# Graph network layer on one core: 72 directly summed columns as three bf16 addends, code copies on POOL, four last groups and a shared last norm

## The chip, the cores and the metric

The kernel runs on one core of a Trainium2 chip. A core has five engines with queues of their own, which run side by side: PE (TensorE, matrix products), DVE (VectorE), ACT (ScalarE), POOL (GpSimd, which also issues the indirect transfers that scatter rows by index) and SP (SyncE, which here issues all other transfers). The metric is the device time of one execution in microseconds, as the median of several runs.

## The reference

206,250 edges carry 128 features each, and 6,250 nodes have 128 features. Every edge's features are added to the node that `src` names; the sums go through three dense layers, and the result plus `x` is normalised over its features. Inputs and output are float32.

```python
edge_aggr = jnp.zeros((n, HIDDEN), dtype=x.dtype).at[row].add(edge_features)
reps = n // global_feat.shape[0]
global_expand = jnp.repeat(global_feat, reps, axis=0)
combined = jnp.concatenate([x, edge_aggr, global_expand], axis=-1) @ W_c + b_c
h = jax.nn.softplus(combined @ W1 + b1)
h = jax.nn.softplus(h @ W2 + b2)
return h @ W3 + b3
...
x = _layernorm(x + _L0_gnn_ref(x, edge_index, edge_attr_128, ...), axis=-1)
```

Negative and out-of-range indices are handled as that scatter-add does it. The edges come in no order that the kernel may rely on.

## The kernel before

**Columns.** The edges are laid over 128 partitions, so that one "column" is 128 edges, one on each; there are 1,612 columns (the last has 42 edges). They are summed in one of two ways.

**Direct columns (48).** `direct_steps` takes them in sets of 12. A set is loaded by one transfer of 768 KB (`load`). For each of 13 windows of 512 nodes (the last has 256) and each pair of columns, ACT makes two 128x512 tables of ones and zeros (`compare`, L577 and L579: is this edge's node this number?), and PE multiplies the rows by them (`add`, L589), in float32, which shows as two records for each product. After the 12 columns of a window DVE adds the result to `sums_t`, the transposed node sums of 128 x 6400 (L593). `compare` runs two steps ahead of `add`; four buffers hold the tables.

**Scattered columns (1,564).** They go through memory in ten groups of `GROUPS`: 40, 120, 200, 240, 240, 240, 212, 140, 88 and 44 columns. The nodes are cut into 25 blocks of 256. For each group:

- `node_codes` (DVE) splits each edge's node into a block and a code inside the block, and `positions` (DVE and PE) counts edges by block and gives every edge a place, so that the edges of one block lie together and each block is padded to a whole number of chunks of `sub` x 128 rows (`sub` is the second number of a group: 1, 2 or 4).
- Pieces of ten columns are loaded by SP (`load_rows`, three pieces ahead, five buffers), ACT copies their ten codes into a 129th value of each row (`code_rows`, L636, issued two pieces ahead), and POOL scatters the rows into a DRAM buffer, one indirect transfer for each column (`scatter_rows`, L644). The DRAM buffer is filled with -1 beforehand (`fill_rows`, on SP), so that padding matches no node.
- `reduce_steps` of the group reads the chunks back, eight chunk columns to a load (SP, L145). DVE compares their codes with 0 to 255 (`match`, L423); PE multiplies the rows by that table (`product`, L437, 256 columns wide, again two records for each); DVE adds each chunk's sum to its block of `sums_t` (L454). In the last two groups (`g > G - 3`) three of every four matches are made by ACT instead (L418 and L420).

**The order of the work.** PE, DVE, ACT and SP have an order written out by hand: while group g is scattered, its loop over pieces deals out, in shares, the preparation of group g+1, the sums of group g-1, the filling for group g+1, the node rows (in groups 3 to 5) and a share of the direct steps (groups 1 to G-4, that is 1 to 6, weighted by `left`). SP's transfers stand in one single order. POOL's queue isn't in that list: the planner places its instructions. The sums of the last group follow after the loop.

**The node layers.** After the last sum, 13 tiles of up to 512 nodes go through the layers. Every few tiles share one `norm`: DVE computes the inverse deviations of all blocks of 128 nodes in a chain of small instructions (L819 to L827), and the blocks are normalised by POOL (L833), in the very last `norm` by DVE. The tiles are parted 4, 3, 3, 2 and 1.

Of the kernel before, what the change touches and what calls it, by code (L numbers as in the profile page):

```python
# [7 lines left out]
F32 = mybir.dt.float32  # L8
# [8 lines left out]
P = 128  # L17
# [4 lines left out]

GROUPS = ((40, 1), (120, 2), (200, 4), (240, 4), (240, 4), (240, 4), (212, 4), (140, 2), (88, 2),
          (44, 1))
CHUNK_ROWS = 1024
PLACES = 3

DIRECT = 48
SET = 12
WIDE = 512  # L30
QUAD = 2
FILL = 4
POS_COLS = 20
# [14 lines left out]
def kernel(  # L48
# [36 lines left out]
    for size, sub in GROUPS:  # L85
        c1 = min(TC, c0 + size)
        if c1 > c0:
# [12 lines left out]

    iota_f = const.tile([P, WIDE], F32, name="iota_f")
    nc.gpsimd.iota(iota_f, pattern=[[1, WIDE]], base=0, channel_multiplier=0,
                   allow_small_or_imprecise_dtypes=True)
# [64 lines left out]
    with ExitStack() as phase:  # L168
# [74 lines left out]
        def positions(g):  # L243
# [5 lines left out]
            in_block, so_far, got = {}, {}, {}  # L249
            pos = per.tile([P, C_MAX], I32, name="pos")  # L250
            pos_of[g] = pos
# [102 lines left out]
            def chunk_map():  # L354

                small = ps.tile([P, 4, P], F32, name="small", bufs=2)
                end_t = per.tile([NB, 1], F32, name="end_t")
                nc.tensor.transpose(small[:NB, 0, :], got["end"], ident)
                nc.vector.tensor_copy(end_t, small[:NB, 0, :1])
                ended = per.tile([NB, NSC_MAX], F32, name="ended")  # L360
                nc.vector.tensor_scalar(ended[:, :nsc], chunk_i[:, :nsc], end_t, None,
                                        op0=ALU.is_ge)
                offs = per.tile([1, NSC_MAX], I32, name="offs", bufs=3)
                offs_of[g] = offs
                flat = ps.tile([P, 4, P], F32, name="small", bufs=2).rearrange("p a b -> p (a b)")
                nc.tensor.matmul(flat[:1, :nsc], ones[:NB, :1], ended[:, :nsc],
                                 start=True, stop=True)
                nc.vector.tensor_scalar(offs[:, :nsc], flat[:1, :nsc], float(NB - 1), float(BL),
                                        op0=ALU.min, op1=ALU.mult)
# [22 lines left out]
        def reduce_steps(g):  # L392
# [16 lines left out]
            def match(i):  # L409
# [3 lines left out]
                hot_of[i] = hot  # L413
                if g > G - 3 and i % 4 != 3:

# [129 lines left out]
        def direct_steps():  # L545


            steps = []
            if not ND:
                return steps  # L550
            NW = -(-NB * BL // WIDE)
            less = keep.tile([P, NW, ND], F32, name="less")
            rows_in, hot_of, sum_of = {}, {}, {}

            def begin():

                first = keep.tile([P, NW], F32, name="first")
                nc.gpsimd.iota(first, pattern=[[WIDE, NW]], base=0, channel_multiplier=0,
                               allow_small_or_imprecise_dtypes=True)
                part, node, _ = whole_nodes(0, ND)  # L560
                nc.vector.tensor_copy(node, part)
                nc.vector.tensor_tensor(
                    less, node.unsqueeze(1).to_broadcast([P, NW, ND]),
                    first.unsqueeze(2).to_broadcast([P, NW, ND]), op=ALU.subtract)

            def load(c):
# [3 lines left out]
                         edge_attr[:P * T, :].rearrange("(p t) d -> p t d", p=P)[:, c:c + n, :])  # L570

            def compare(c, w, q):
                n = min(WIDE, NB * BL - w * WIDE)
                hot = direct_p.tile([P, QUAD, WIDE], F32, name="direct_hot", bufs=4)
                hot_of[c, w, q] = hot
                for j in range(QUAD):
                    nc.scalar.activation(hot[:, j, :n], iota_f[:, :n], AF.Abs,  # L577
                                         bias=less[:, w, c + q + j:c + q + j + 1], scale=-1.0)
                nc.scalar.activation(hot[:, :, :n], hot[:, :, :n], AF.Relu, bias=ones[:, :1],  # L579
                                     scale=-1.0)  # L580

            def add(c, w, q):
# [3 lines left out]
                if q == 0:  # L586
                    sum_of[c, w] = ps.tile([P, WIDE], F32, name="direct_sum", bufs=2)
                for j in range(QUAD):
                    nc.tensor.matmul(sum_of[c, w][:, :n], rows_in[c][:, q + j, :], hot[:, j, :n],  # L589
                                     start=(q + j == 0), stop=(q + j == k - 1))  # L590
                if q + QUAD == k:
# [4 lines left out]
                    for q in range(0, min(SET, ND - c), QUAD)]  # L596
            steps += [begin, lambda: load(0)]
            for i in range(len(jobs) + 2):
                def one(i=i):
                    if i < len(jobs):  # L600
                        c, w, q = jobs[i]
                        if (w, q) == (NW // 2, 0) and c + SET < ND:
                            load(c + SET)
                        compare(*jobs[i])
                    if i > 1:
# [26 lines left out]
        def code_rows(i):  # L632
            if i >= len(pieces):
                return
            g, c, k, r = pieces[i]
            nc.scalar.copy(rows_at[i][:r, :k, D:W], low[:r, c:c + k].unsqueeze(2))  # L636

# [14 lines left out]
        with tc.manual_schedule(engines={ET.PE, ET.DVE, ET.Activation, ET.SP}):  # L652
# [22 lines left out]
            node_codes(ND, c1)  # L675
            for i in range(LEAD - 1):
                code_rows(i)
            for step in positions(0):
# [11 lines left out]
            left = [0.0] * G  # L690
            for g in range(1, G - 3):
                left[g] = max(0.0, groups[g][1] - groups[g][0]
                              - groups[g - 1][3] * groups[g - 1][2] / 3 - (9 if 3 <= g < 6 else 0))
            direct_at = 0.0
            i = 0
            assert G > 6
            nodes = []
            for g in range(G):
                mine = [q for q in range(len(pieces)) if pieces[q][0] == g]
                prep = []  # L700
                if g + 1 < G:
                    prep = [lambda g=g: node_codes(*groups[g + 1][:2])] + positions(g + 1)
                sums = reduce_steps(g - 1) if g else []
# [7 lines left out]
                done = [0, 0, 0, 0]  # L711
                for q in mine:
                    load_rows(i + LEAD)
                    code_rows(i + LEAD - 1)
                    scatter_rows(i)
# [30 lines left out]
    order = tiles[-1:] + tiles[:-1]  # L746
    parts = [order[:4]] + [order[i:i + 3] for i in range(4, len(order) - 3, 3)]
    parts += [order[len(parts) * 3 + 1:-1], order[-1:]]
    h1, h2, sub_z, x_of = {}, {}, {}, {}
# [64 lines left out]
    def norm(now, last):  # L814
# [9 lines left out]
        for _ in range(3):  # L824
            nc.vector.tensor_mul(t, g, g)
            nc.vector.scalar_tensor_tensor(t, t, -0.5, v, op0=ALU.mult, op1=ALU.mult)
            nc.vector.scalar_tensor_tensor(g, t, 1.5, g, op0=ALU.add, op1=ALU.mult)  # L827

        engine = nc.vector if last else nc.gpsimd
        for n0, w, y, at in now["done"]:  # L830
            for lo, hi, r in blocks(w):
                for q in range(lo, hi):
                    engine.tensor_scalar(y[:r, q, :], y[:r, q, :], mv[:r, at + q, 0:1],  # L833
                                         rs[:r, 1, at + q:at + q + 1],
                                         op0=ALU.subtract, op1=ALU.mult)
                m0 = n0 + lo * P
# [60 lines left out]
```

## Time and profile before

| What | Value |
|---|---|
| time, median of 3 runs | 2163.95 us (2160.82 to 2169.29) |
| the profiled execution's own time | 2166.67 us |
| its span | 2164.9 us |
| mean granted PE clock | 0.925 |
| first scatter | 25.57 us |
| PE busy from 1188 to 1296, and from 1296 to 1404 | 98.7 and 92.0 of 108 us |
| POOL busy in the same two | 81.9 and 82.0 of 108 us (86 scatters each) |
| ACT waiting for PE's direct products | 808.1 us in 199 waits |
| SP waiting for PE's chunk products | 885.2 us in 214 waits |
| last matmul of the sums ends / first of the node layers starts | 2084.1 / 2086.1 us |

All lines are of one execution. A busy share is an average over stages with different limits: what decides in a stretch is the engine whose instructions follow each other there without a wait. In a group of instructions, "busy, mean ns of one" comes first and then the idle time of the engine just before them, with what ended it; "issue" is time in which the engine waited for nothing that the profile shows. In a timeline the columns are start, duration, engine, line, operation, output and inputs, count, and in brackets the idle time before with what ended it.

### The profile page before, as it was taken

The page shows a single profiled execution, that of the slowest core. Times are in us where ns is not written, and L with a number is a line of the kernel's source. Part 1 is how long each engine was busy: PE and PEld are TensorE (multiplying, and loading weights), DVE is VectorE, ACT ScalarE, POOL GpSimd, SP SyncE. Part 2 cuts the span into 40 slices and gives each one's busy share as a digit, 9 for nine tenths or more (in the row PEclk, how much of TensorE's full clock was granted, in tenths as well). Part 3 has the DMA queues.
Part 4 walks back from the last instruction along what each step waited for, and adds up shares of the span by engine and source line. Part 5 has one row for each costly group of instructions (what it writes and reads, how often), then busy time and mean ns, then how long its engine had stood idle before and what let it go on. Part 6 is the DMA issues. An engine that isn't in the chain of part 4 may idle for free.

```text
span 2164.9 us, 22230 instructions
## 1 busy us (share of the span) xinstructions
PE 1789.7 (83%) x6415; PEld 1209.0 (56%) x6415; DVE 1328.0 (61%) x1923; ACT 912.7 (42%) x1350; POOL 1560.2 (72%) x1631
## 2 busy tenths in 40 slices
PE   3398788966889878999889998788998899688884
PEld 0144445534555555666556666556666778566752
DVE  7386457524656345675465855355755798796567
ACT  0476665653444335444353443353342000006964
POOL 5777777777777767777777777777777777777226
PEclk8699999987999999999999999999999999899997
DMA  9998788738786665676756666556766687776521
GB/s 299 303 313 270 216 256 251 231 101 262 213 225 189 194 193 148 188 207 188 198 173 180 194 190 175 169 167 189 202 198 170 211 245 227 214 213 199 151 75 60
DMA packets 415376, 435.50 MB, mean 201 GB/s; under 512 B 37743, under 2 KB 305766, under 8 KB 415254
## 3 DMA queue, kind: packets, MB, share of 16 engines
q1 hardware_dynamic: 365062, 330.71, 54.9%
q0 software_dynamic: 50048, 103.35, 14.4%
q8 instruction: 51, 0.84, 0.2%
q14 instruction: 71, 0.58, 0.1%
q10 hardware_dynamic: 144, 0.02, 0.0%
HBM read 260.90 MB, written 173.03 MB: 200 GB/s over the span
## 4 chain that ended last, share of the span: by engine, by line
PE 57%; DVE 15%; POOL 9%; issue 7%; DMA 6%; ACT 4%; DVEq 1%; SPq 0%; POOLq 0%; ACTq 0%
PE part L437 37%; PE direct_sum L589 16%; POOL place L644 8%; DVE hot L423 7%; DMA place<-rows,pos 4%; DVE sums_t L454 2%; ACT hot L418 2%; DVE so_far L316 1%; DVE sums_t L593 1%; DMA rows<-in_edge_attr 1%; DMA chunks<-place 1%; PE small L339 1%; POOL y L833 1%; DVEq L448 1%; DVE pos L350 1%
## 5 line engine op out<-in xcount | busy, mean ns | idle before, releaser
L644 POOL DMA_INDIRECT place<-rows,pos x1564 | 1503.2, 961 | 509.0 <-issue 443.5
L437 PE MATMUL part<-hot,chunks 128*128 128x256 f32 x4472 | 1106.0, 405 | 267.8 <-DVE hot L423 250.9
L437 PEld LDWEIGHTS part<-hot,chunks 128*128 128x128 f32 x4472 | 894.9, 203 | 507.8 <-DVE hot L423 310.5
L577 ACT ACTIVATE direct_hot<-iota_f,less 128x512 f32<-128x512 f32 (+1 forms) x624 | 404.6, 695 | 811.0 <-PE direct_sum L589 808.1
L423 DVE SCALAR_TENSOR_TENSOR hot<-chunks,iota_ps 128x2048 f32<-128x2048 f32 (+1 forms) x261 | 592.2, 2270 | 44.2 <-DMA chunks<-place 44.2
L589 PE MATMUL direct_sum<-direct_hot,direct_rows 128*128 128x512 f32 (+1 forms) x1248 | 559.0, 580 | 29.4 <-DMA direct_rows<-in_edge_attr 25.6
L454 DVE TENSOR_TENSOR sums_t<-sums_t,part 128x256 f32 x781 | 327.1, 419 | 133.3 <-PE part L437 110.8
L589 PEld LDWEIGHTS direct_sum<-direct_hot,direct_rows 128*128 128x128 f32 x1248 | 233.3, 190 | 232.2 <-issue 204.9
L579 ACT ACTIVATE direct_hot<-direct_hot,ones 128x1024 f32<-128x1024 f32 (+1 forms) x312 | 348.0, 1115 | 10.1
L593 DVE TENSOR_TENSOR sums_t<-sums_t,direct_sum 128x512 f32<-128x512 f32 (+1 forms) x52 | 34.7, 667 | 410.5 <-PE direct_sum L589 410.5
L636 ACT COPY rows<-src_i 128x10 f32<-128x10 f32 (+1 forms) x159 | 30.7, 196 | 360.3 <-DMA place<-rows,pos 328.9
L350 DVE TENSOR_REDUCE pos<-at 128x20 int32<-128x500 f32 (+2 forms) x80 | 87.0, 1087 | 2.7
L316 DVE TENSOR_TENSOR_SCAN so_far<-iota_ps,ib 128x1500 bf16<-128x1500 f32 (+5 forms) x29 | 85.7, 2955 | 0.0
L418 ACT ACTIVATE hot<-iota_f,chunks 128x256 f32<-128x256 f32 x156 | 64.2, 493 | 26.7 <-DMA chunks<-place 24.2
L845 POOL TENSOR_TENSOR x_sb<-x_sb,b_all 128x512 f32<-128x512 f32 (+1 forms) x13 | 15.2, 1219 | 67.8 <-DMA x_sb<-in_x 67.8
L348 DVE TENSOR_TENSOR at<-small,ib 128x500 f32<-128x500 f32 (+2 forms) x80 | 52.9, 661 | 4.2 <-PE small L339 3.5
L833 POOL TENSOR_SCALAR y<-y,mv,rs 128x128 f32<-128x128 f32 (+1 forms) x45 | 35.2, 796 | 19.9 <-DVE rs L827 19.0
L262 DVE TENSOR_TENSOR ib<-block,iota_ps 128x1500 bf16<-128x1500 bf16 (+5 forms) x29 | 44.2, 1550 | 0.0
L273 PE MATMUL small<-ib,ones_h 128*128 128x500 bf16 (+2 forms) x80 | 23.8, 406 | 23.9 <-DVE ib L262 23.9
L536 DVE TENSOR_SCALAR z_x<-small,z_bias 128x512 f32<-128x512 f32 (+1 forms) x13 | 9.3, 718 | 51.3 <-PE small L534 51.3
L335 PE MATMUL small<-so_far,ones_h 128*128 128x500 bf16 (+2 forms) x80 | 31.4, 393 | 11.1 <-DVE last L319 11.1
L420 ACT ACTIVATE hot<-hot,ones 128x2048 f32<-128x2048 f32 (+1 forms) x20 | 39.2, 1960 | 0.7
(115 smaller groups left out, 472.7 us busy)
## 6 DMA issues: line engine op xcount, KB each, us to landing
chunks<-place SPq DMA_DIRECT2D x278, 516.0 KB, 4.5
rows<-in_edge_attr SPq DMA_DIRECT2D x155, 640.0 KB, 6.7
place<-fill SPq DMA_DIRECT2D x252, 258.0 KB, 8.3
place<-rows,pos POOLq DMA_INDIRECT x1564, 4.5
x_sb<-in_x SPq DMA_DIRECT2D x24, 256.0 KB, 4.6
direct_rows<-in_edge_attr SPq DMA_DIRECT2D x4, 768.0 KB
out<-y SPq DMA_DIRECT2D x12, 256.0 KB, 2.2
chunks<-place SPq DMA_DIRECT2D x3, 258.0 KB, 3.2
```

The source lines that it names most:

```text
L316: nc.vector.tensor_tensor_scan(t, iota_ps[:, 1:2].to_broadcast([P, NB * n]), in_block[k][0], 0.0, op0=ALU.mult, op1=ALU.add)
L350: nc.vector.tensor_reduce(pos[:, a - c0 + j0:a - c0 + j1], at.rearrange("p b g -> p g b"), axis=mybir.AxisListType.X, op=ALU.add)
L418: nc.scalar.activation(hot[:, j], codes, AF.Abs, bias=chunks[i][:, j, D:W], scale=-1.0)
L423: nc.vector.scalar_tensor_tensor(hot[:, :m], chunks[i][:, :m, D:W].to_broadcast([P, m, BL]), code_of(g), iota_ps.unsqueeze(1).to_broadcast ...
L437: nc.tensor.matmul(part[:, s - q, :], t[:, s * sub + j, :D], hot[:, s * sub + j], start=(j == 0), stop=(j == sub - 1))
L454: nc.vector.tensor_add(here, here, part[:, s - q, :])
L577: nc.scalar.activation(hot[:, j, :n], iota_f[:, :n], AF.Abs, bias=less[:, w, c + q + j:c + q + j + 1], scale=-1.0)
L579: nc.scalar.activation(hot[:, :, :n], hot[:, :, :n], AF.Relu, bias=ones[:, :1], scale=-1.0)
L589: nc.tensor.matmul(sum_of[c, w][:, :n], rows_in[c][:, q + j, :], hot[:, j, :n], start=(q + j == 0), stop=(q + j == k - 1))
L593: nc.vector.tensor_add(here, here, sum_of.pop((c, w))[:, :n])
L644: s = nc.gpsimd.indirect_dma_start(out=dst, out_offset=bass.IndirectOffsetOnAxis(ap=at, axis=0), in_=rows[:r, j, :], in_offset=None)
L833: engine.tensor_scalar(y[:r, q, :], y[:r, q, :], mv[:r, at + q, 0:1], rs[:r, 1, at + q:at + q + 1], op0=ALU.subtract, op1=ALU.mult)
```

## The change

It does five things at once.

1. **72 direct columns instead of 48**, and their products in bf16. A new step `split` (DVE) writes each float32 value as a sum of three bf16 values: its upper 16 bits, the upper 16 bits of what is left, and the rest of that. The first two stand in place in the loaded rows (every second bf16 value of them), the third in a tile of its own. PE multiplies each of the three by the same table, which is now bf16, and adds them in float32 in PSUM. `split` works on two columns at a time, three DVE instructions of 128x256. The difference of node and window start (`less`) is made for a set at a time, and the tables have three buffers after four. The first set's load is issued at the end of group 0, its `begin` and `split` at the start of group 1.
2. **POOL copies the codes** (`code_rows`), called just ahead of the piece's scatters, instead of ACT two pieces ahead.
3. **The last groups** are 202, 130, 72, 38 and 18 columns instead of 212, 140, 88 and 44: eleven groups, 1,540 scattered columns. Direct steps still lie in groups 1 to 6. Matches go to ACT in the last three groups, by `TAIL`: one of two, three of four, three of four.
4. **Positions one group sooner** from group 6 on: group 6 prepares groups 7 and 8, group 7 prepares 9, group 8 prepares 10, with a third `pos` and a fourth `offs` buffer.
5. **The last norm is shared** by the last three tiles (parts of 4, 3, 3 and 3): half of its blocks are normalised by DVE and half by ACT.

```diff
-GROUPS = ((40, 1), (120, 2), (200, 4), (240, 4), (240, 4), (240, 4), (212, 4), (140, 2), (88, 2),
-          (44, 1))
+GROUPS = ((40, 1), (120, 2), (200, 4), (240, 4), (240, 4), (240, 4), (202, 4), (130, 2), (72, 2),
+          (38, 1), (18, 1))
+SOONER = 6
+TAIL = (2, 4, 4)
-DIRECT = 48
+DIRECT = 72
+SPLIT = 2
...
-            pos = per.tile([P, C_MAX], I32, name="pos")
+            pos = per.tile([P, C_MAX], I32, name="pos", bufs=3)
...
-                if g > G - 3 and i % 4 != 3:
+                share = TAIL[g - G] if g >= G - len(TAIL) else 1
+                if i % share != share - 1:
...
+            def halves(t):
+                return [t.bitcast(BF16).rearrange("p c (d h) -> p c d h", h=2)[:, :, :, h]
+                        for h in (0, 1)]
+
+            def split(c):
+                n = min(SET, ND - c)
+                less = less_of[c] = direct_p.tile([P, NW, SET], F32, name="less", bufs=2)
+                nc.vector.tensor_tensor(
+                    less[:, :, :n], node_f[:, c:c + n].unsqueeze(1).to_broadcast([P, NW, n]),
+                    first.unsqueeze(2).to_broadcast([P, NW, n]), op=ALU.subtract)
+                low_in[c] = direct_p.tile([P, SET, D], BF16, name="direct_low", bufs=2)
+                for a in range(0, min(SET, ND - c), SPLIT):
+                    b = min(a + SPLIT, SET, ND - c)
+                    rest = direct_p.tile([P, SPLIT, D], F32, name="direct_rest")[:, :b - a]
+                    x_c = rows_in[c][:, a:b]
+                    nc.vector.tensor_sub(rest, x_c, halves(x_c)[1])
+                    nc.vector.tensor_sub(low_in[c][:, a:b], rest, halves(rest)[1])
+                    nc.vector.tensor_copy(halves(x_c)[0], halves(rest)[1])
...
-                hot = direct_p.tile([P, QUAD, WIDE], F32, name="direct_hot", bufs=4)
+                hot = direct_p.tile([P, QUAD, WIDE], BF16, name="direct_hot", bufs=3)
...
-                for j in range(QUAD):
-                    nc.tensor.matmul(sum_of[c, w][:, :n], rows_in[c][:, q + j, :], hot[:, j, :n],
-                                     start=(q + j == 0), stop=(q + j == k - 1))
+                for j in range(q, q + QUAD):
+                    addends = halves(rows_in[c][:, j:j + 1]) + [low_in[c][:, j:j + 1]]
+                    for i, part in enumerate(addends):
+                        nc.tensor.matmul(sum_of[c, w][:, :n], part[:, 0], hot[:, j - q, :n],
+                                         start=(j == 0 and i == 0), stop=(j == k - 1 and i == 2))
...
+                        if (w, q) == (NW - 2, 0) and c + SET < ND:
+                            split(c + SET)
...
-            nc.scalar.copy(rows_at[i][:r, :k, D:W], low[:r, c:c + k].unsqueeze(2))
+            nc.gpsimd.tensor_copy(rows_at[i][:r, :k, D:W], low[:r, c:c + k].unsqueeze(2))
...
-                if g + 1 < G:
-                    prep = [lambda g=g: node_codes(*groups[g + 1][:2])] + positions(g + 1)
+                for k in range(g + 1 + (g > SOONER), min(G, g + 2 + (g >= SOONER))):
+                    prep += [lambda k=k: node_codes(*groups[k][:2])] + positions(k)
...
+                    if g == 0 and q == mine[-1]:
+                        for step in direct_first:
+                            step()
                     load_rows(i + LEAD)
-                    code_rows(i + LEAD - 1)
+                    code_rows(i)
                     scatter_rows(i)
...
-    parts = [order[:4]] + [order[i:i + 3] for i in range(4, len(order) - 3, 3)]
-    parts += [order[len(parts) * 3 + 1:-1], order[-1:]]
+    parts = [order[:4]] + [order[i:i + 3] for i in range(4, len(order), 3)]
...
+                    if last and q % 2:
+                        nc.scalar.activation(y[:r, q, :], y[:r, q, :], AF.Identity,
+                                             bias=minus[:r, k:k + 1], scale=g[:r, k:k + 1])
+                        continue
```

More of the change, by code (lines that the diff above doesn't have):

```diff
@@ L98 @@
     dram = ctx.enter_context(tc.tile_pool(name="dram", bufs=1, space=bass.MemoryType.DRAM))
-    iota_f = const.tile([P, WIDE], F32, name="iota_f")
-    nc.gpsimd.iota(iota_f, pattern=[[1, WIDE]], base=0, channel_multiplier=0,
+    iota_f = const.tile([P, len(TAIL) * BL], F32, name="iota_f")
+    nc.gpsimd.iota(iota_f, pattern=[[1, len(TAIL) * BL]], base=0, channel_multiplier=0,
                    allow_small_or_imprecise_dtypes=True)
@@ L362, in chunk_map @@
                                         op0=ALU.is_ge)
-                offs = per.tile([1, NSC_MAX], I32, name="offs", bufs=3)
+                offs = per.tile([1, NSC_MAX], I32, name="offs", bufs=4)
                 offs_of[g] = offs
@@ L551, in direct_steps @@
             NW = -(-NB * BL // WIDE)
-            less = keep.tile([P, NW, ND], F32, name="less")
-            rows_in, hot_of, sum_of = {}, {}, {}
+            node_f = keep.tile([P, ND], F32, name="node_f")
+            first = keep.tile([P, NW], F32, name="first")
+            less_of = {}
+            rows_in, low_in, hot_of, sum_of = {}, {}, {}, {}
             def begin():
-                first = keep.tile([P, NW], F32, name="first")
                 nc.gpsimd.iota(first, pattern=[[WIDE, NW]], base=0, channel_multiplier=0,
                                allow_small_or_imprecise_dtypes=True)
[L560 to L564, printed above, removed]
+                part, _, _ = whole_nodes(0, ND)
+                nc.vector.tensor_copy(node_f, part)
             def load(c):
@@ L577, in compare @@
                     nc.scalar.activation(hot[:, j, :n], iota_f[:, :n], AF.Abs,
-                                         bias=less[:, w, c + q + j:c + q + j + 1], scale=-1.0)
+                                         bias=less_of[c][:, w, q + j:q + j + 1], scale=-1.0)
                 nc.scalar.activation(hot[:, :, :n], hot[:, :, :n], AF.Relu, bias=ones[:, :1],
@@ L596, in direct_steps @@
                     for q in range(0, min(SET, ND - c), QUAD)]
-            steps += [begin, lambda: load(0)]
+            steps += [lambda: load(0), begin, lambda: split(0)]
             for i in range(len(jobs) + 2):
@@ L632, in code_rows @@
         def code_rows(i):
-            if i >= len(pieces):
-                return
             g, c, k, r = pieces[i]
-            nc.scalar.copy(rows_at[i][:r, :k, D:W], low[:r, c:c + k].unsqueeze(2))
+            nc.gpsimd.tensor_copy(rows_at[i][:r, :k, D:W], low[:r, c:c + k].unsqueeze(2))
         def scatter_rows(i):
@@ L675 @@
             node_codes(ND, c1)
-            for i in range(LEAD - 1):
-                code_rows(i)
             for step in positions(0):
@@ L690 @@
             left = [0.0] * G
-            for g in range(1, G - 3):
+            for g in range(1, G - 4):
                 left[g] = max(0.0, groups[g][1] - groups[g][0]
                               - groups[g - 1][3] * groups[g - 1][2] / 3 - (9 if 3 <= g < 6 else 0))
+            direct_first = direct[:1]
+            direct = direct[1:]
             direct_at = 0.0
@@ L827, in norm @@
             nc.vector.scalar_tensor_tensor(g, t, 1.5, g, op0=ALU.add, op1=ALU.mult)
-        engine = nc.vector if last else nc.gpsimd
+        if last:
+            minus = work.tile([P, 16], F32, name="minus")[:, :nb]
+            nc.vector.scalar_tensor_tensor(minus, mv[:, :nb, 0], -1.0, g,
+                                           op0=ALU.mult, op1=ALU.mult)
         for n0, w, y, at in now["done"]:
@@ L832, in norm @@
                 for q in range(lo, hi):
-                    engine.tensor_scalar(y[:r, q, :], y[:r, q, :], mv[:r, at + q, 0:1],
-                                         rs[:r, 1, at + q:at + q + 1],
-                                         op0=ALU.subtract, op1=ALU.mult)
+                    k = at + q
+                    if last and q % 2:
+                        nc.scalar.activation(y[:r, q, :], y[:r, q, :], AF.Identity,
+                                             bias=minus[:r, k:k + 1], scale=g[:r, k:k + 1])
+                        continue
+                    (nc.vector if last else nc.gpsimd).tensor_scalar(
+                        y[:r, q, :], y[:r, q, :], mv[:r, k, 0:1], g[:r, k:k + 1],
+                        op0=ALU.subtract, op1=ALU.mult)
                 m0 = n0 + lo * P
```

## The prediction

> **What bounds the kernel now.** I read four views in this order: engine shares, groups of instructions, waits, then POOL's and DVE's timelines at the places that the change touches.
>
> ```profile
> PE 1789.7 (83%) x6415; PEld 1209.0 (56%) x6415; DVE 1328.0 (61%) x1923; ACT 912.7 (42%) x1350; POOL 1560.2 (72%) x1631
> POOL 5777777777777767777777777777777777777226
> L644 POOL DMA_INDIRECT place<-rows,pos x1564 | 1503.2, 961 | 509.0 <-issue 443.5
> L437 PE MATMUL part<-hot,chunks 128*128 128x256 f32 x4472 | 1106.0, 405 | 267.8 <-DVE hot L423 250.9
> L589 PE MATMUL direct_sum<-direct_hot,direct_rows 128*128 128x512 f32 (+1 forms) x1248 | 559.0, 580 | 29.4 <-DMA direct_rows<-in_edge_attr 25.6
> L636 ACT COPY rows<-src_i 128x10 f32<-128x10 f32 (+1 forms) x159 | 30.7, 196 | 360.3 <-DMA place<-rows,pos 328.9
> ```
>
> PE has the largest share, but the flat row of sevens on POOL is the bound: a scatter is 0.96 us busy and then 0.30 us "issue", in which it waits for nothing, in slice after slice. The timeline shows what that makes, and where it breaks.
>
> ```profile
> 801.28 0.96 POOL L644 DMA_INDIRECT place<-rows,pos  x1 [0.30 <-issue]
> 811.52 0.96 POOL L644 DMA_INDIRECT place<-rows,pos  x1 [9.28 <-ACT rows L636]
> ...
> 1851.44 0.97 POOL L644 DMA_INDIRECT place<-rows,pos  x1 [0.30 <-issue]
> 1852.71 0.96 POOL L644 DMA_INDIRECT place<-rows,pos  x1 [0.30 <-issue]
> ...
> 2018.42 0.91 POOL L644 DMA_INDIRECT place<-rows,pos  x1 [0.30 <-issue]
> ```
>
> From 1852.71 to 2018.42 lie the 132 scatters of the last two groups: 165.7 / 131 = 1.265 us each. From 81 us on POOL stopped once, 9.28 us at 811.52, for a code copy that stood behind ACT's other work. So the span is 25.6 us of start, 1564 scatters at 1.265, two early stops, 66.6 us from the last scatter to the last sum, and 79 us of node layers:
>
> ```profile
> 1893.62 2.28 DVE L423 SCALAR_TENSOR_TENSOR hot<-chunks,iota_ps 128x2048 f32<-128x2048 f32 x1
> 1897.58 2.28 DVE L423 SCALAR_TENSOR_TENSOR hot<-chunks,iota_ps 128x2048 f32<-128x2048 f32 x1
> ...
> 2032.44 3.29 ACT L418 ACTIVATE hot<-iota_f,chunks 128x256 f32<-128x256 f32 x8
> 2035.76 2.00 ACT L420 ACTIVATE hot<-hot,ones 128x2048 f32<-128x2048 f32 x1
> ...
> 2084.08 1.86 DVE L454 TENSOR_TENSOR sums_t<-sums_t,part 128x256 f32 x4 [0.20 <-DVE sums_t L454]
> ```
>
> In the tail POOL is no longer the limit. A load of 8 chunk columns costs 3.96 us where DVE does every match (the 140 group), 5.23 us on ACT (2032.44 to 2037.67), and the 44 group took 41.3 us (2044.6 to 2085.9) for 8.5 loads, 4.86 each.
>
> **The change, part by part.** Time T7 is the first scatter of the group of 88 (72 afterwards), 1852.7 now.
>
> *24 columns fewer are scattered.* Up to T7 it is 20 (1432 to 1412): 20 x 1.265 = -25.3 us. *ACT leaves POOL's path*: the 9.28 us stop goes, -9.3.
>
> *Code copies on POOL.* 142 pieces precede T7. Their source, destination and neighbours wait for nothing new: they write only the code column, and in the built program each stands one piece (ten scatters) ahead of its scatters, so those find it done. But POOL's time is the bound, and no trace row shows a POOL copy. Bounds: below, the four one-column memsets start 0.03 us apart. Above, a 13-column iota's 0.14 plus a second issue gap of 0.30, some 0.45. The nearest row is that iota:
>
> ```profile
> 1.35 0.12 POOL L105 IOTA part_f<- 128x1 f32 x1
> 1.44 0.21 POOL L667 IOTA chunk_i<- 25x94 f32 x1
> 6.98 0.14 POOL L558 IOTA first<- 128x13 f32 x1
> ```
>
> Ten strided numbers are near 0.14, and 1.35 to 1.44 shows that dispatch hides behind the work before it: I take 0.15. 142 x 0.15 = +21.3 (4 to 64 by the bounds). T7 becomes 1852.7 - 25.3 - 9.3 + 21.3 = 1839.4.
>
> *Direct sums.* A float32 product of 512 columns is two records in 0.86 us (4 records take 1.72 us start to start); the bf16 position products of 500 columns (L334 to L336) start 0.21 apart with their 0.10 us weight loads hidden. So 12.5 windows x 72 columns x 3 x 0.215 = 581 us on PE instead of 12.5 x 48 x 0.86 = 516: +65 over groups 1 to 6. Per 240-column group that makes PE's work some 263 us after 251 (336 chunk columns x 0.431 = 145, direct 98 after 85, the rest positions and node rows), against 304 (then 308) of POOL. ACT makes a pair of columns in 2.41 us (starts at 95.60, 98.02, 100.43): 36 x 12.5 x 2.41 = 1085 us instead of 723, in a window of 1242 x 1.265 = 1571; in the 120 group it is 159 us against 152, the only place where it reaches POOL. DVE gains 36 pairs of columns x 3 operations of 128x256 at 0.42 = 45 us, 26 sums x 0.67 = 17, and 6 small subtractions, at 0.6 to 0.7 busy. All this is off the path, cost 0, because the row loads cover it: in the two timelines SP issues a piece's load 40 to 60 us ahead of its first scatter (24 at the worst, once, at 1651), and landing takes 7. If PE fell 30 us behind, POOL would stop for what is beyond that. SP's queue changes little: two more direct loads of 768 KB, the first moved ahead of two row loads that have 35 us in hand; POOL has only the copies. The third "pos" and fourth "offs" buffer let the 130 and 72 groups' positions be prepared in group 6 (DVE there 187 us of 259, my count), so none is late.
>
> *The new subtractions read SBUF twice.* Such instructions already run beside scatters: at 817.84, beside the node preparation (L199, 0.41 us), a scatter took 0.99 instead of 0.96. 72 x 0.03 = 2 us, taken as 0.
> The Trainium skill (SBUF — State Buffer, section "SBUF: two separate sides") says that VectorE and GpSimd share one pair of SBUF ports by an exclusive lock, and that a VectorE instruction with two SBUF inputs shuts out a GpSimd one that reads SBUF for its whole length. Were that so for every scatter, 72 locks of 0.41 us would add 30 us and the sum would show almost no gain; the row at 817.84 is against it, and only a POOL copy that happens to meet one could pay.
>
> *Tail.* T8 = 1839.4 + 72 x 1.265 + 8 x 0.15 = 1931.7. The 130 group's sums start 5.9 us after T7 (as 1858.64 does), take 178/8 = 22.25 loads x 3.96 = 88 us of DVE, plus some 10 for the positions of 18 columns: 1943. They are then 12 us behind POOL, so PE starts the 72 group at about 1945 (T8 + 10.8 is the earliest, as 1974.8 was). There every second load is matched by ACT: a pair costs ACT 5.23, DVE 2.2 + 2 x 1.85 = 5.9, PE 2 x 3.45 = 6.9, so PE decides: 15 x 3.45 = 52, until 1997. The 38 group: 62/8 = 7.75 x 4.86 = 38, until 2035; the 18 group: 5.25 x 4.86 = 25.5, until 2060. The last scatter ends near 2004, 56 us before, so it hides. Last sum 2085.9 to 2060.2: -25.7.
>
> *Last norm shared.* Tiles 11 to 13 get one norm: the eight-block one's small DVE chain (2148.27 to 2150.95) goes, 2.7 us, and twelve blocks are split, six at 0.35 = 2.1 on DVE beside ACT, where four took 1.4; the POOL norm that ended at 2157.45 is gone. The end moves from there to about 2155.1: -2.3 (0 to -4).
>
> Sum: 2164.9 - 25.7 - 2.3 = 2136.9 span, plus 1.8 outside it (2166.67 - 2164.9) = 2138.7. That execution is 2.7 above the median of the runs, so I say 2138.
>
> **Rivals.**
> (a) The copy costs its own issue gap, 0.45: 150 copies that count x 0.30 more = +45, 2183. For it: every POOL entry in the steady stretch has that gap. Against: the gaps between other POOL instructions at the start are zero. Above 0.32 a copy the change loses; above 0.395 by over 0.5%.
> (b) Copies almost free, 0.03: -17, 2121. For: the 0.30 us of issue could hide all of a 0.14 us copy. Against: nothing shows that issue and work overlap.
> (c) Weight loads of every second bf16 value are not hidden: 2808 x 0.10 = +281 us on PE; by the count above groups 1 to 6 then need 1338 + 281 = 1619 us of PE against 1242 x 1.265 + 127 x 0.15 = 1590 of POOL. So +29, 2167, and up to 2200 where DVE's waits add to it. For: no such strided load is in the trace. Against: L334 to L336.
> (d) It does little: copies between 0.25 and 0.395, 2153 to 2175.
>
> **How the numbers follow.** Forecast (copy 0.08 to 0.25, 2126 to 2153) 0.53, (b) 0.16, (d) 0.13, (a) 0.09, (c) 0.09. No change is within 0.5%, about what can be told from none here: 2153 to 2175. Faster 0.53 + 0.16 = 0.69; same 0.13 and a little of (c), 0.15; slower 0.16. The range 2118 to 2174 leaves out (a), the dearer half of (c), and a few hundredths below; the forecast's own is 2126 to 2153.
>
> **What would show it.** The POOL copies' mean and the spacing of the scatters on both sides of one: over 1.55 us together is (a), 1.30 is (b). Spacing still 1.265 elsewhere; no stop near 811. Direct matmul records 0.215 apart: if 0.3, (c). SP's row loads still over 30 us ahead in groups 4 to 6. Last scatter near 2004, last sum near 2060, span less last sum about 77. Wrong: scatters that lengthen beside the new subtractions, or POOL stopping for rows or positions.

## The result, and the profile after

The changed kernel takes 2244.4 us (median of 4, 2243.3 to 2252.8), the kernel before 2163.4 beside it: ratio 1.0383, 95% interval 1.0363 to 1.0402. It is 81 us slower, where 2138 was forecast. The profiled execution took 2252.8 us, with a span of 2251.0 and a mean granted clock of 0.956. Most of the runs below (all but a3, g1 and m1) fell on chips on which every kernel, the one before too, takes some 30% longer (it took 2,829 to 2,854 us there). On them ACT and DVE show 1,122 to 2,249 us of waits that the profile calls "remote" and puts down to nothing on the core, where the runs on the other chips show 0 to 7. These runs are given as ratios to the kernel before on the same chip (what is in brackets behind a ratio is its 95% interval), and the cause of the 81 us does not rest on them.

The page of the changed kernel, busy shares, POOL's slices, the chain that ended last, and the two groups that matter:

```profile
PE 1853.8 (82%) x7867; PEld 1240.2 (55%) x7977; DVE 1392.2 (62%) x2104; ACT 1247.5 (55%) x1654; POOL 1562.2 (69%) x1756
POOL 5677777777777777567677777677656477777415
...
PE 51%; DVE 21%; POOL 7%; ACT 7%; issue 6%; DMA 5%; DVEq 1%; SPq 1%; ACTq 0%; POOLq 0%
...
L676 POOL DMA_INDIRECT place<-rows,pos x1540 | 1480.6, 961 | 594.4 <-issue 406.6
L624 DVE TENSOR_TENSOR sums_t<-sums_t,direct_sum 128x512 f32<-128x512 f32 (+1 forms) x78 | 52.0, 667 | 553.2 <-PE direct_sum L620 546.0
```

POOL's row of sevens now has fives and sixes in its second half: it no longer scatters without a pause. Its waits, and those of SP's queue, which loads the rows:

```profile
POOL place L676 <- issue: 406.6, 1333, 0.4
POOL place L676 <- DMA rows<-in_edge_attr: 107.9, 28, 19.6
...
POOL place L676 <- DVE pos L356: 13.4, 4, 5.4
POOL place L676 <- DVE hot L430: 10.9, 3, 6.1
```

```profile
SPq L151 <- PE part L444: 1020.4, 246, 9.1
SPq L151 <- DVE hot L430: 387.6, 92, 31.0
SPq L151 <- DMA place<-rows,pos: 126.2, 29, 12.7
```

POOL waits 107.9 us for rows that have not landed. SP is late with them because its queue also loads the chunks, and a chunk load stands until PE or DVE gives a buffer free: 1408 us in all. Only 126 us of SP's time does it wait for POOL to empty a row buffer, which is the wait that it has when it is ahead. One piece as an example, in POOL's timeline and in SP's:

```profile
1012.15 0.21 POOL L668 COPY rows<-src_i 128x10 f32<-128x10 f32 x1
1013.79 0.98 POOL L676 DMA_INDIRECT place<-rows,pos  x1 [1.43 <-DMA rows<-in_edge_attr]
```

```profile
1006.16 0.37 SPq L151 DMA_DIRECT2D rows<-in_edge_attr  x1
```

The load goes out 7.6 us ahead of its first scatter: its lead is the landing time and nothing more. Matched issue by issue with the pieces, the lead (from a load's issue to the first scatter of its piece) falls from 40 to 50 us in most of group 2 to 7 at the end of group 3, and stays at 6 to 18 for most of groups 4 to 6. The first scatters of the groups say what that costs: groups 4, 5 and 6 take 340, 325 and 320 us; at 1.265 us a scatter their 240, 240 and 202 columns would take 304, 304 and 256.

Why PE and DVE are late shows in DVE's timeline, and in PE's beside it:

```profile
969.48 0.69 DVE L624 TENSOR_TENSOR sums_t<-sums_t,direct_sum 128x512 f32<-128x512 f32 x1 [12.36 <-PE direct_sum L620]
970.08 0.67 DVE L354 TENSOR_TENSOR at<-small,ib 128x500 f32<-128x500 f32 x1
970.78 1.09 DVE L356 TENSOR_REDUCE pos<-at 128x20 int32<-128x500 f32 x1
971.80 2.27 DVE L430 SCALAR_TENSOR_TENSOR hot<-chunks,iota_ps 128x2048 f32<-128x2048 f32 x1
```

```profile
969.92 0.59 PE L620 MATMUL direct_sum<-direct_hot,direct_rows 128*128 128x512 bf16 x2
970.35 0.38 PE L620 MATMUL direct_sum<-direct_hot,direct_low 128*128 128x512 bf16 x1
974.12 5.41 PE L444 MATMUL part<-hot,chunks 128*128 128x256 f32 x16 [3.39 <-DVE hot L430]
```

DVE stands 12.36 us with nothing to do, because the next instruction in its queue adds a window's direct sum (L624), and PE has not made the last products of that window. The match for the next chunks (L430) is written behind it, so it starts only at 971.80; PE is through with its direct products at 970.73 and then idles 3.39 us for that match. Each waits for the other in turn. In groups 4, 5 and 6 DVE stands 13, 12 and 11 times for window sums (101, 88 and 83 us), and PE 18, 19 and 19 times for matches (40.5, 32.6 and 49.6 us).

### The profile page after: what moved, and what is told of

Its sections match the earlier page's. It is cut to its first block, busy times and chain, and to the rows that moved or that the text cites. A ratio compares the mean times of both kernels' runs of the same rounds, so it can differ in the third digit from the quotient of the medians.

```text
span 2251.0 us, 25230 instructions
## 1 busy us (share of the span) xinstructions
PE 1853.8 (82%) x7867; PEld 1240.2 (55%) x7977; DVE 1392.2 (62%) x2104; ACT 1247.5 (55%) x1654; POOL 1562.2 (69%) x1756
## 4 chain that ended last, share of the span: by engine, by line
PE 51%; DVE 21%; POOL 7%; ACT 7%; issue 6%; DMA 5%; DVEq 1%; SPq 1%; ACTq 0%; POOLq 0%
PE part L444 33%; PE direct_sum L620 15%; DVE hot L430 8%; POOL place L676 7%; DVE sums_t L461 3%; DVE so_far L322 3%; ACT direct_hot L606 2%; ACT direct_hot L608 2%; DMA place<-rows,pos 2%; DMA place<-fill 2%; DVE sums_t L624 2%; SPq L151 1%; DVE pos L356 1%; DVE at L354 1%; DVEq L455 1%
## 5 line engine op out<-in xcount | busy, mean ns | idle before, releaser
L676 POOL DMA_INDIRECT place<-rows,pos x1540 | 1480.6, 961 | 594.4 <-issue 406.6
L606 ACT ACTIVATE direct_hot<-iota_f,less 128x512 bf16<-128x512 f32 (+1 forms) x936 | 604.7, 693 | 695.9 <-PE direct_sum L620 634.1
L430 DVE SCALAR_TENSOR_TENSOR hot<-chunks,iota_ps 128x2048 f32<-128x2048 f32 x263 | 595.6, 2266 | 0.0
L620 PE MATMUL direct_sum<-direct_hot,direct_rows 128*128 128x512 bf16 (+1 forms) x1775 | 519.5, 371 | 91.9 <-ACT direct_hot L608 60.6
L608 ACT ACTIVATE direct_hot<-direct_hot,ones 128x1024 bf16<-128x1024 bf16 (+1 forms) x468 | 521.9, 1115 | 15.2
L624 DVE TENSOR_TENSOR sums_t<-sums_t,direct_sum 128x512 f32<-128x512 f32 (+1 forms) x78 | 52.0, 667 | 553.2 <-PE direct_sum L620 546.0
L620 PE MATMUL direct_sum<-direct_hot,direct_low 128*128 128x512 bf16 (+1 forms) x923 | 342.9, 372 | 4.5
L620 PEld LDWEIGHTS <-direct_rows 128*128 128x128 bf16 x1872 | 180.3, 98 | 299.2 <-issue 98.3
L620 PEld LDWEIGHTS <-direct_low 128*128 128x128 bf16 x936 | 91.4, 98 | 103.6 <-issue 1.1
L322 DVE TENSOR_TENSOR_SCAN so_far<-iota_ps,ib 128x1500 bf16<-128x1500 f32 (+7 forms) x30 | 84.6, 2819 | 0.0
L268 DVE TENSOR_TENSOR ib<-block,iota_ps 128x1500 bf16<-128x1500 bf16 (+7 forms) x30 | 43.8, 1483 | 0.0
L341 PE MATMUL small<-so_far,ones_h 128*128 128x500 bf16 (+2 forms) x79 | 31.1, 393 | 10.5 <-DVE last L325 10.5
```

The source lines that it names most:

```text
L322: nc.vector.tensor_tensor_scan(t, iota_ps[:, 1:2].to_broadcast([P, NB * n]), in_block[k][0], 0.0, op0=ALU.mult, op1=ALU.add)
L430: nc.vector.scalar_tensor_tensor(hot[:, :m], chunks[i][:, :m, D:W].to_broadcast([P, m, BL]), code_of(g), iota_ps.unsqueeze(1).to_broadcast ...
L606: nc.scalar.activation(hot[:, j, :n], iota_f[:, :n], AF.Abs, bias=less_of[c][:, w, q + j:q + j + 1], scale=-1.0)
L620: nc.tensor.matmul(sum_of[c, w][:, :n], part[:, 0], hot[:, j - q, :n], start=(j == 0 and i == 0), stop=(j == k - 1 and i == 2))
L624: nc.vector.tensor_add(here, here, sum_of.pop((c, w))[:, :n])
L676: s = nc.gpsimd.indirect_dma_start(out=dst, out_offset=bass.IndirectOffsetOnAxis(ap=at, axis=0), in_=rows[:r, j, :], in_offset=None)
```

## The experiments

Three parts could make the rows late: the 24 columns, POOL's copies, and the place of the window sums in DVE's queue. The runs undo them singly and together.

**e1: the copies alone.** The kernel before, `code_rows` on POOL.

```diff
...
-            nc.scalar.copy(rows_at[i][:r, :k, D:W], low[:r, c:c + k].unsqueeze(2))
+            nc.gpsimd.tensor_copy(rows_at[i][:r, :k, D:W], low[:r, c:c + k].unsqueeze(2))
...
-                    code_rows(i + LEAD - 1)
+                    code_rows(i)
```

> The kernel before with one edit: POOL copies the codes just ahead of a piece's scatters. The main theory (the changed kernel loses its time because PE and DVE, not POOL, set the pace from the fourth group on) expects that the copies alone cost about 0.1 us each: 159 x 0.1 = 16 us, less the 9 us stop at 811 us that ACT caused, so 2164 to 2178 us and no stop of POOL for rows. The rival that the copies are what costs the time expects over 2220 us.

Two repeats, r1 and f4:

> The kernel before with nothing changed but its code copies, made by POOL just ahead of a piece's scatters. If a copy costs POOL the 0.06 to 0.28 us that the pieces of the changed kernel show, and the stop of 9.3 us for ACT goes: 157 x 0.06 to 0.28 less 9.3 = 0 to 35 us more than before, ratio 1.000 to 1.016. If the copies are what makes the changed kernel slow: at least 1.035, with POOL starved of nothing.

> The kernel before with nothing changed but its copies, made by POOL. Theory that a copy costs POOL 0.06 to 0.28 us and nothing else: 2160 less 9 plus 9 to 44, so 2160 to 2195. Rival, that giving up the hold which ACT's copies keep on ACT (which waits 329 us there for places to be scattered) disturbs the order: over 2200, with late rows on POOL.

Measured: 1.0485 of the kernel before (1.0392 to 1.0578), 1.0518 (1.0403 to 1.0632) and 1.0390 (1.0296 to 1.0485). All on the slower chips, where POOL waits 653 to 693 us for late rows: far more than the copies' own time, 159 x 0.21 us. That is the outcome that the rival of f4 names (the order is disturbed when ACT no longer stands for its copies). It was not tried on the other chips.

**e4: positions prepared one group ahead everywhere**, as before (`SOONER = 99`, two `pos` buffers).

> The changed kernel with positions prepared one group ahead throughout, as before (group 6 prepares group 7 alone). The theory that two preparations in group 6 make it late (it takes 320 us for 202 columns, where the 240 columns of group 5 take 325) expects 25 to 45 us gained, 2200 to 2220 us. The main theory (direct sums) expects a gain of some 10 us, given back in group 7, 2235 to 2245 us.

Measured: 1.1127 (1.1028 to 1.1227), on a slower chip, where the changed kernel itself has 1.1065 on another (r0). The two intervals overlap, so nothing is seen to be won by it there. That the earlier positions are not what costs on the other chips follows from m1 and g1 below, which keep them.

**r0: the changed kernel unedited** on a slower chip.

> The changed kernel unedited, as the measure for the other kernels of this group, since the chip of the first four runs was some 30% slower than that of the comparison. On a chip like that of the comparison: 2243 to 2253 us, 1.038 of the kernel before. If a slower chip changes how late rows and waits fall, the ratio is another one, and then only ratios within this group are used.

Measured: 1.1065 (1.0970 to 1.1159). The ratio there is another than 1.038, so a ratio from those chips cannot be carried over.

**e5: 48 direct columns, still in bf16 addends, copies on POOL.**

```diff
-GROUPS = (..., (202, 4), (130, 2), ...)
+GROUPS = (..., (226, 4), (130, 2), ...)
...
-DIRECT = 72
+DIRECT = 48
```

> The changed kernel with 48 direct columns, in bf16 addends, and 24 columns more in group 6 (226). The main theory (the direct sums of the 24 columns push PE and DVE beyond POOL's pace) expects that POOL waits for rows under 15 us in all and the time is 2130 to 2165 us, although 24 scatters (30 us) come back. The rivals that leave the direct sums out of it (copies, last groups, early positions) expect 2244 + 30 = 2274 us or at least no gain.

Repeats r2 and f2:

> The changed kernel with 48 direct columns, in bf16 addends (group 6 takes the 24 columns back). Theory (72 columns are too much work for the order in which PE, DVE and ACT go, so the row loads' lead is used up): the lead stays, POOL waits for late rows under 20 us in all, ratio to before 0.985 to 1.005. Rival (the bf16 addends themselves, their splitting or the copies make it slow): late rows stay, 1.02 or more.

> The changed kernel with 48 direct columns, still in bf16 addends and with POOL's copies. Theory (24 columns): late rows on POOL under 20 us, 2135 to 2175. Rival (POOL's copies): 2190 or more.

Measured: 1.0629 (1.0484 to 1.0775), 1.0610 (1.0537 to 1.0682) and 1.0445 (1.0345 to 1.0544), with 555 to 636 us of POOL's waits for late rows. Late rows that stay, at 1.02 or more, are what the rival of r2 said; but there the copies alone make rows late (e1), so this does not tell the addends, their splitting and the copies apart. On the chip of r0 and r2 some 4% go with the 24 columns (1.061 after 1.1065).

**a1: the code copies back on ACT**, 72 columns kept.

```diff
...
-            nc.gpsimd.tensor_copy(rows_at[i][:r, :k, D:W], low[:r, c:c + k].unsqueeze(2))
+            nc.scalar.copy(rows_at[i][:r, :k, D:W], low[:r, c:c + k].unsqueeze(2))
...
-                    code_rows(i)
+                    code_rows(i + LEAD - 1)
```

> The changed kernel with the code copies given back to ACT (seven pieces ahead, as before). Theory that the copies on POOL cost it 0.06 to 0.28 us each and the late rows come from PE, DVE and ACT being behind: POOL waits for late rows as long as with POOL's copies, and some copies behind ACT's longer queue come late too: ratio to the kernel before 1.03 to 1.06 where the changed kernel has 1.038, or 1.09 to 1.13 on a chip where it has 1.107. Rival, that the copies on POOL are the larger half: at most 1.02, or 1.06 where the changed kernel has 1.107.

A repeat, f1:

> The changed kernel with the code copies given back to ACT, on a chip that runs the kernel before in about 2161 us. Theory that 24 more direct columns make PE, DVE and ACT slower than POOL, so that the row loads come late whoever makes the copies: 2230 to 2275 us, 1.03 to 1.05 of the kernel before. Rival, that the copies on POOL are the larger half of the loss, as the ratios on the slow chips say: 2150 to 2200, 0.995 to 1.02.

(LEAD is 3: the copies go two pieces ahead, not seven, as in the kernel before.)

Measured: 1.0324 (1.0232 to 1.0416) on a slower chip, a time as the rival said. POOL still stands there, now 719.6 us for ACT's copies and 68.9 for rows, where it stood 709.4 for rows in r0. The two runs of f1, 2918 and 2976 us after 2854 for the kernel before, are too far apart for a ratio. The kernel was not measured on the other chips.

**e2, and again m1: the window sums four direct steps later**, everything else of the change kept.

```diff
                 if q + QUAD == k:
-                    here = sums_t[:, w * WIDE:w * WIDE + n]
-                    nc.vector.tensor_add(here, here, sum_of.pop((c, w))[:, :n])
+                    whole.append((c, w, n))
+            whole = []
+            def add_window():
+                c, w, n = whole.pop(0)
+                here = sums_t[:, w * WIDE:w * WIDE + n]
+                nc.vector.tensor_add(here, here, sum_of.pop((c, w))[:, :n])
...
-            for i in range(len(jobs) + 2):
+            for i in range(len(jobs) + 6):
...
-                    if i > 1:
+                    if 1 < i < len(jobs) + 2:
                         add(*jobs[i - 2])
+                    if whole and (i >= len(jobs) + 5 or (i > 5 and i < len(jobs) + 6 and jobs[i - 6][2] + QUAD == min(SET, ND - jobs[i - 6][0]))):
+                        add_window()
```

> The changed kernel, in which DVE adds the sum of a direct window four steps later, so that it no longer stands in its queue waiting for the window's last product while the next matches wait behind it. The main theory (order: 546 us of DVE waits at the window sums delay the matches, and PE then waits for them) expects that most of POOL's 108 us for late rows go: 2140 to 2175 us. The rival that PE simply has too much work (1338 us in groups 1 to 6 by the count, plus what its waits add) expects less than 25 us gain: 2220 to 2245 us.

Repeats r3, f3, h1 and k1:

> The changed kernel with each window's sum of the direct columns added by DVE four direct steps later than now, so that DVE does not stand in its queue for a PSUM sum whose last products PE has yet to make. Theory that this wait in the written order is what costs PE its pace: DVE's idle time ahead of the window sums falls from 546 us to under 250, and the time by 40 us or more, ratio to the changed kernel of this group 0.955 to 0.98. Theory that the amount of work sets the pace whatever the order: within 1% of the changed kernel.

> The changed kernel with the window sums of the direct columns added four direct steps later. If DVE's standing for these sums is what lets PE fall behind: late rows on POOL under 50 us of the 108, DVE's wait ahead of the sums under 250 us of 546, and 2150 to 2205 us. If the amount of work sets the pace: 2230 to 2250.

> The changed kernel with only the window sums added four direct steps later; POOL keeps its copies. The run with both (ACT's copies too) took 2118. If the order of the window sums is the cause of the late rows: no late rows, and 2118 plus what the copies cost POOL, 142 x 0.06 to 0.28 = 9 to 40, so 2127 to 2158. If ACT's hold by its copies is what keeps the order together: late rows stay, 2190 or more.

> The changed kernel with only the window sums added four direct steps later; POOL keeps its copies. On a chip that runs the kernel before in about 2161 us: if the order of the window sums is the cause of the late rows, none are late, and 2118 (both edits) plus what the copies cost POOL, 142 x 0.06 to 0.28 = 9 to 40, gives 2127 to 2158. If ACT's copies are what keeps the order together: late rows stay, 2190 or more.

Measured on the slower chips: 1.0886 (1.0760 to 1.1012), and 1.0779, 1.0769, 1.0738 and 1.0796 in the repeats. DVE's wait for PE's products ahead of the sums falls as expected (465 us in r0, 62 to 100 in these five), and r3 takes 0.974 of r0 on the same chip, inside what the theory of the order said. Late rows remain there (623 to 699 us), so on those chips the order of the sums is not the whole cause. The run m1 is from a chip that does the kernel before in 2170.2:

> The changed kernel with only the window sums added four direct steps later; POOL keeps its copies. On a chip that runs the kernel before in about 2161 us: if the order of the window sums is the cause of the late rows, none are late, and 2118 (both edits) plus what the copies cost POOL, 142 x 0.06 to 0.28 = 9 to 40, gives 2127 to 2158. If ACT's copies are what keeps the order together: late rows stay, 2190 or more. On a chip 30% slower for all kernels: 1.07 to 1.09 of the kernel before, as three times now, and nothing new.

Measured: 2133.6 us, ratio 0.9830 (0.9788 to 0.9872), where the theory of the order said 2127 to 2158. This one edit turns 81 us of loss into 37 us of gain. So on these chips there is no such loss without the waits at the window sums. Whether they alone make it, or only together with the 24 columns and POOL's copies, is not shown: neither was undone here with the order left as it was. m1's group of window sums, SP's waits, and DVE at the same place of the program:

```profile
L630 DVE TENSOR_TENSOR sums_t<-sums_t,direct_sum 128x512 f32<-128x512 f32 (+1 forms) x78 | 51.8, 664 | 70.5 <-PE direct_sum L620 68.2
```

```profile
SPq L151 <- DMA place<-rows,pos: 1050.8, 280, 12.4
SPq L151 <- PE part L444: 379.8, 120, 6.0
...
SPq L151 <- DVE hot L430: 19.0, 10, 4.2
```

```profile
980.78 1.11 DVE L356 TENSOR_REDUCE pos<-at 128x20 int32<-128x500 f32 x1
981.81 0.68 DVE L630 TENSOR_TENSOR sums_t<-sums_t,direct_sum 128x512 f32<-128x512 f32 x1
982.40 2.28 DVE L430 SCALAR_TENSOR_TENSOR hot<-chunks,iota_ps 128x2048 f32<-128x2048 f32 x1
```

The idle time ahead of the window sums falls from 553 to 70 us; the add goes through at 981.81 without a wait, and the match follows at once. SP's waits have changed sides: 1051 us for POOL to empty a buffer, 399 for PE and DVE. No wait of POOL for rows is left among its longest, and the row loads' lead stands at 48 to 50 us in groups 4 and 5: four pieces of 12.7 us, which is all that five buffers allow. Group 5 in the changed kernel (1143 to 1468) and in m1 (1106 to 1412; columns: length, then busy time of PE, PEld, DVE, ACT and POOL, granted clock, DMA share, GB/s):

```profile
1143.00:1468.00 325.00, 283.98 (x1223) 191.00 (x1242) 188.17 (x239) 189.49 (x241) 236.18 (x266) 0.95 0.61 174
```

```profile
1106.00:1412.00 306.00, 276.12 (x1248) 185.41 (x1247) 187.92 (x237) 197.04 (x250) 235.98 (x266) 0.98 0.58 182
```

The same work within some 8 us on every engine, 19 us apart. PE waits for matches 10.5 us in group 5 after 32.6; for ACT's tables 8.5 after 6.6, so the third table buffer that the change took away is not what held it.

**a3: 48 columns in bf16, copies on ACT, later window sums** (the edits of e5, a1 and e2 together; of the change the addends, the last groups and the norm remain).

> Of the change only the bf16 addends for 48 columns, the last groups of 130, 72, 38 and 18 (226 in group 6) and the shared norm are kept; ACT makes the code copies as before; and the window sums of the direct columns are added four steps later. Theory that 24 more columns and the order are what costs: the tail's gain comes through, ratio to the kernel before 0.97 to 0.99. Rival, that the bf16 addends themselves (their splitting, 36 small DVE operations fewer than with 72 columns) cost what they save: 0.995 to 1.02.

Measured: 2148.5 us, 0.9945 (0.9923 to 0.9968), between the two expectations: less gain than the tail promised.

**g1: 72 columns, copies on ACT, later window sums.**

> The changed kernel with its 72 columns, the code copies given back to ACT and the window sums added four steps later. With 48 columns so arranged (2148) DVE waited 341 us for chunks to match and the row loads kept 49 us of lead; 24 columns more add some 194 us of PE, 60 of DVE's splits and sums. Theory that order and copies are what costs: the lead stays over 30 us, and 24 x 1.265 = 30 us come off: 2110 to 2130. Theory that 72 columns are too much work in any order: late rows, 2190 or more.

Measured: 2118.1 us, 0.9770 (0.9741 to 0.9798). So 72 columns are not too much work: 24 columns more than in a3 take 30.4 us off, and 24 x 1.265 is 30.4. That the two agree so closely is luck, since the runs are from two chips: by the ratios it is some 38 us, give or take 8. The traces have it in its place: group 6, of 226 and 202 columns, takes 285.4 us in a3 and 255.4 in g1. It is the fastest of all kernels here, 126 us below the changed kernel by the medians. Against m1 it also bounds the price of POOL's copies, since the rest is the same: 15.5 us in all, again between two chips. Of the 14.0 us that m1 is behind at the first scatter of the 72 group (1834.2 after 1820.2), 4.1 arise before the second group starts, where POOL stands 9.6 us for a load after 6.2 in g1; the other 9.9 over 138 copies are 0.07 us each. One copy in m1:

```profile
1308.97 0.95 POOL L684 DMA_INDIRECT place<-rows,pos  x1 [0.30 <-issue]
1309.91 0.22 POOL L676 COPY rows<-src_i 128x10 f32<-128x10 f32 x1
1310.29 0.98 POOL L684 DMA_INDIRECT place<-rows,pos  x1 [0.15 <-POOL rows L676]
```

The copy takes 0.22 us, but it lies in the 0.30 us in which POOL issues the next scatter anyway: from scatter to scatter 1.32 us instead of 1.265.

## Why the prediction was wrong

**The step that failed** is "All this is off the path, cost 0, because the row loads cover it". It cost 114 us up to the first scatter of the 72 group (1953.3, where the sum has 1839.4), as much as the whole error. Three things were wrong with it.

- *The sum was of busy times, without the waits that the order forces.* 263 us of PE against 304 of POOL in a 240 group looked like 41 us to spare. The count itself was low: in groups 4 and 5 PE is busy 276 to 277 us in m1, and 265 to 279 in the kernel before, for which it has 251. In the changed kernel PE was busy 284 to 289 there, and idle 41 to 51 more, 33 to 41 of it standing for DVE's matches. The 26 added window sums were counted as work (17 us of DVE), not as places in DVE's queue where it must wait for PE with the next matches behind it. m1 moves those places alone and has 306 us for the group, POOL's pace. The kernel before had such waits already, 410.5 us of DVE in its row of window sums; in its group 5 PE is busy 264.6 us and waits 36.2 for matches, 300.8 of the 303.6 that the group takes. That group had little to spare even before the change:

```profile
L593 DVE TENSOR_TENSOR sums_t<-sums_t,direct_sum 128x512 f32<-128x512 f32 (+1 forms) x52 | 34.7, 667 | 410.5 <-PE direct_sum L589 410.5
```

- *The cover was read too large.* "40 to 60 us ahead (24 at the worst)" was off by one piece and more: counted issue by issue, the kernel before has 29 to 55 us in group 4 (38 in the mean), 22 to 50 in group 6, and 14 for the load at 1661. In the changed kernel group 3 alone used it up: the lead fell from 36 us at its first piece to 7 at its last.
- *The profile of before had the sign.* Its SP queue waited 885.2 us for PE's chunk products and 207.7 for DVE's matches, but only 365.2 for POOL's buffers. SP waits for its consumer in m1 (1051 us), where it is far ahead, and mostly for other engines' buffers where it has little to give. The first of these numbers stood in the table of the profile before, and was not read so:

```profile
SPq L145 <- PE part L437: 885.2, 214, 12.0
SPq L145 <- DMA place<-rows,pos: 365.2, 104, 12.0
SPq L145 <- DVE hot L423: 207.7, 56, 18.5
```


**The other steps**, which m1 shows without the stall (span 2130.5; the prediction's 2136.9):

- *20 and 24 columns at 1.265 us*: right. Groups 4 and 5 of g1 take 304 us for 240 scatters each, and group 6 is 30.0 us shorter in g1 than in a3 for its 24 columns fewer.
- *The 9.3 us stop for ACT goes*: right; in the changed kernel the scatters from 809 to 822 stand 1.26 to 1.28 apart, and 1.33 across the copy.
- *The copy at 0.15 us*: mis-sized, 0.07. It hides in the issue gap, which is the mechanism of rival (b), whose 0.03 was too little. Rival (a) is out.
- *Direct products 0.215 apart, weight loads hidden*: right (in the timeline of m1 two products start from 961.25 on, the third at 961.68, the fourth at 961.89). Rival (c) is out as a mechanism; the 98 ns loads cost nothing, though its outcome, PE as the pace, came by another way.
- *The first scatter of the 72 group* at 1839.4: 1834.2 in m1.
- *The tail* from there to the last sum, 220.8: 225.3 in m1 and 228.0 in the changed kernel. The new last groups do what was worked out to within 5 to 7 us.
- *The shared norm* at -2.3: mis-sized. From the last sum to the end are 71.0 us in m1 and 70 in the changed kernel, after 79.0. About 4 of it lie before the last norm ends (67.6 us after the last sum instead of 71.5), and 4 behind it (3.4 us of output instead of 7.4), which the prediction did not count at all.
- *The subtractions beside the scatters*: 0.03 us each was taken as 0. In m1 a split from 962.2 to 969.3 lengthens three of five scatters to 1.08, 1.13 and 1.16 us, 0.49 together, some 3 us over six splits. The Trainium skill (SBUF — State Buffer, "SBUF: two separate sides") has a VectorE instruction with two SBUF inputs and a GpSimd instruction that reads SBUF shut each other out for the whole instruction. For the indirect transfers these rows do not show that: twelve such instructions of 0.42 us lie in that stretch, two of them wholly inside a scatter that took its usual 0.96 us, and together they cost at most a tenth of their length.

That m1's span comes within 6.4 us of the sum is in part luck: 5.2 too many up to the 72 group, 4.5 too few in the tail, 5.7 too many behind the last sum. And by its own words the sum gives 2136.0 for the median (2138.7 less 2.7), where 2138 was said.

None of the rivals was this one. The right rival was: DVE's queue stands for more window sums, PE for DVE, SP for PE, POOL for SP, with the price of the lead that runs out.

## What to carry to other kernels

Where engines run in an order written out by hand, an engine's reserve is not its pace less its busy time: count the places where one queue must stand for another, what is queued behind each, and move such waits some steps behind the work that ends them (four steps were worth 111 us here by the medians, and 118 counted against the kernel before on each chip). Look also at the loader's own waits: in the runs here, waiting for the consumer's buffers went with a lead of 48 to 50 us (m1), waiting for other engines' with one of 38 (before) or 6 to 18 (after).

## What was not expected of the hardware

- In m1 a POOL copy of 0.22 us costs 0.07 between two indirect transfers: it runs within the 0.30 us that otherwise pass before the next one.
- On the slower chips the instructions of POOL, DVE and ACT take as long as elsewhere (in r0 a scatter 0.96 us, a match 2.27), and PE's a little longer (422 ns after 404 for a record of a chunk's product, at a granted clock of 0.82 after 0.96). But DVE and ACT have waits that end by nothing on the core (in r0 of up to 84 us), and PE stands up to 27 us at "issue". POOL's copies lose 4 to 5% there alone (e1 and its repeats), where elsewhere they cost 15.5 us of 2118, and giving them back to ACT helped more there (1.107 to 1.032) than the later window sums (to between 1.074 and 1.089). Why is open: the kernel before was not profiled on such a chip, and POOL's copies alone, or ACT's copies with the order of the window sums unchanged, were not tried on the others.
